# Layer 2's second half routed by rows of the batch, with layer 3's mixers, routes and experts queued in a new order behind it

## The chip, the cores and the metric

The kernel runs on one core of a Trainium2 chip, in one launch. The metric is the device time of an execution in microseconds (us), as the median of several runs. "The span" is the time between the first and the last event of one profiled execution. Times given as positions ("at 1664") are microseconds from the start of that span.

## The reference, cut to what matters

The input x has 4 batch rows of 1024 tokens with 128 features, in fp32. Four layers follow each other. Each layer is a mixer over tokens and then a feed-forward part (FFN), and behind each of the eight steps stands x = layernorm(x + step(x)). The change touches the last two layers:

```
# layer 2, mixer: causal attention with 16 heads of 8 features, inside one batch row
attn = softmax(where(tril, q @ k.T / sqrt(8), -inf));  out = (attn @ v) @ Wo.T + Wo_b
# layer 2, FFN: 8 experts (F = 512), the best 2 of each token by softmax(x @ gate_w.T)
# layer 3, mixer: over the FIRST axis (the 4 batch rows), for each token position by itself
n, b, e = query.shape                      # (4, 1024, 128)
x = query / (norm(query) * e ** -0.5 + 1e-8)
u = silu(x @ u_w.T + u_b);  v = silu(x @ v_w.T + v_b)          # 256 features, 8 heads
y = toeplitz over n of v (7 lags for each head)
out = (u * y) @ o_w.T + o_b + query
# layer 3, FFN: 32 experts (F = 128), the best 4 of each token, and one shared FFN (F = 512)
```

What matters for the order of the work: attention of layer 2 needs all earlier tokens of its own batch row, and no other row. The mixer of layer 3 needs all four batch rows at the same token position, and no other position. The FFNs work on each token alone.

## The kernel before, in words

**Tiles.** x stays on the chip's SBUF as 32 tiles of 128 tokens. They are kept in quarters of the sequence: a quarter is 256 tokens of each of the four rows, so 8 tiles (`tile_of`, `quarter`). A `Part` is a run of quarters: part a is quarters 0 and 1 (16 tiles), b is quarter 2 and c is quarter 3 (8 tiles each).

**Attention of layer 2** (`l2_attn(hf)`) runs in two halves of the sequence. Its second half goes row by row through the batch: 26 units for each row, each with score matmuls on TensorE, two exps on ScalarE (L1032, 128×1024 each) and value matmuls. The steps that close a row (`finish`: `turn`, `back`, `out`, `routed`, `logits`) and those that prepare the next row are put into a list `todo` and worked off between units. `logits` (L2's router) writes into `l2_lg`.

**An expert FFN** has these steps. A route (`l2_route`, `l3_route`, with `positions`, L1212 on) works out, mostly on VectorE (DVE), for each token the places in a list in DRAM sorted by expert. `spread` (L1280) has GpSimd (POOL) write each tile's x rows to those places by an indirect DMA, k per tile for the best k experts. `gathered` (L1294) loads groups of 512 list rows on SyncE's (SP's) queue, and waits for all scatters of the list. The experts (`l2_experts`, `small_experts`) multiply block by block with weights from one tile `wall`, loaded by `l2_wall` or `l3_wall`, and store the results to a second list. `collect` reads them back by k indirect gathers per tile on POOL (L1334) and adds them to x, weighted, on DVE (L1327). A list of layer 2 for 8 tiles has 24 blocks of 128 rows, that of layer 3 has 24 groups of 512 rows for part a and 16 each for b and c.

**Order.** All functions are generators, which yield an estimate of the microseconds that they have just queued. `mix(main, side)` (L210) advances the side by as many estimated microseconds as the main part has yielded. Side instructions are kept, by a dependency without a semaphore, behind the last instruction that the main part has queued on the same engine. What is left of the side when main is done is queued after it (`drain=True`) or is kept for the next mix (`drain=False`). Each engine works off its own queue in order. The scheduler of the framework may still move instructions without such a dependency within a queue. Tiles in SBUF come from pools on a stack at the left and one at the right edge. A tile that lies where a closed pool's tile was waits for the last use of that tile.

**The schedule from the second half of layer 2's attention on** (`all`, L1767 to L1781):

```python
run(self.mix(self.l2_attn(1), self.between(a, True)))
...
    routed = self.chain(self.routed(b), self.routed(c))
    run(self.mix(self.l3_experts(a, self.l3_wall(c2)), routed))
...
    run(self.mix(self.l2_experts(b, wall), self.last(a)))
    on = self.between(b)
    run(self.mix(self.l2_experts(c, wall), on, drain=False))
```

`between(part)` is layer 2's `collect`, then `l3_attn`, `l3_route` and `spread` of layer 3. So beside attention, part a goes through the rest of layer 2 and layer 3's mixer. Then part a's experts of layer 3 run, with the routing of layer 2's b and c beside them. Then come layer 2's experts of b (beside them `last(a)`, the gathers of layer 3's part a) and of c (beside them `between(b)`). Then layer 3 goes on for the rest: `l3_shared(a)`, shared and experts of b beside `between(c)`, shared and experts of c beside `finish(a)` (a layernorm and the stores of the output), `last(b)` and `finish(b)`; at the end `last(c)` and `finish(c)`. `l3_attn` has a form `exps`, used beside attention: it makes silu from Tanh and takes the square roots on DVE, so that ScalarE's exps keep their table. The plain form uses Silu and Sqrt on ScalarE.

Of the kernel before, what the change touches and what calls it, by code (L numbers as in the profile page):

```python
# [15 lines left out]
ALU = mybir.AluOpType  # L16
# [46 lines left out]
class Part:  # L63


    def __init__(self, name, q0, nq):
        self.name, self.q0, self.nq = name, q0, nq
        self.t0, self.nt = q0 * QT, nq * QT

    def tiles(self, x):  # L70
        return x[:, self.t0 : self.t0 + self.nt, :]
# [7 lines left out]
class Kernel:  # L79
    def __init__(self, ctx, tc, ins, out, cols, consts, rows):  # L80
# [34 lines left out]
        self.parts = (self.first, *self.rest)  # L115

        self.lists, self.route = {}, {}
        self.both = (self.first, Part("r", 2, 2))
        for lay, ne, k in (("l1", E1, K1), ("l2", E2, K2), ("l3", E3, K3)):
            for pt in self.both if lay == "l1" else self.parts:  # L120
                tl = -(-((pt.nt * P * k + (P - 1) * ne) // P) // 4) * 4
                self.lists[lay, pt.name] = (
                    self.tile(dram, [tl * P, D], f"{lay}r{pt.name}"), self.tile(dram, [tl * P, D], f"{lay}y{pt.name}"), tl
                )
# [19 lines left out]
    def load(self, pool, src, eng=None, tag=None):  # L144
        t = self.tile(pool, list(src.shape), tag or f"ld{next(self.count)}")
# [662 lines left out]
    def l1_close(self, part, yp):  # L808

        nc, x = self.nc, self.x  # L810
        for q in range(part.q0, part.q0 + part.nq):
            yield from self.collect("l1", part, K1, yp, part.tiles(x), (q - part.q0) * QT, QT)
# [43 lines left out]
    def l2_logits(self, ps, t4, lg, tag):  # L856
# [4 lines left out]
        self.nc.vector.tensor_copy(lg, pl.rearrange("p (q k) e -> p q k e", k=2))  # L861

    def l2_attn(self, hf):
# [6 lines left out]
        with ExitStack() as ctx:  # L870
            kv = self.pool(ctx, "l2kv")
            w = self.load(kv, self.ins["l2_w"])
# [15 lines left out]
            tp = self.pool(ctx, "l2t", 2)  # L888
# [49 lines left out]
            def finish(b, oc):  # L938
# [38 lines left out]
                def logits():  # L977
                    lg = self.l2_lg.rearrange("p (q b k) e -> p b q k e", q=NQT, b=B)[:, b, 2 * hf : 2 * hf + 2]
                    self.l2_logits(ps_m, made["t4"], lg, "s")
# [64 lines left out]
            def values_of(u, prs):  # L1044
# [13 lines left out]
                for m in [m for m in pos if ends[m][-1] == i]:  # L1058
                    t = self.tile(bp, [P, BLK], "oc", bufs=5)
# [41 lines left out]
            values_of(*late.pop(0))  # L1101
            for step in todo:
                step()
                yield (2.0,)
            if hf == 0:
                nc.sync.dma_start(out=self.vsave, in_=va)
                nc.sync.dma_start(out=self.ksave, in_=kT)

    def l2_attn_general(self):
# [3 lines left out]
        with ExitStack() as ctx:  # L1113
# [88 lines left out]
            for q in range(NQT):  # L1202
                self.norm(self.quarter(q))
                for g in range(2):
                    t0 = q * QT + g * 4
                    lg = self.l2_lg[:, t0 : t0 + 4, :].rearrange("p (q k) e -> p q k e", k=2)
                    t4 = self.tile(pp, [P, BLK], "t4")
                    self.transposes(ps_t, t4, [x[:, t0 + k, :] for k in range(4)], on_act=False)
                    self.l2_logits(ps_t, t4, lg, "tp")
# [64 lines left out]
    def spread(self, lay, part, k):  # L1274
# [3 lines left out]
        for t in range(part.nt):  # L1278
            for i in range(k):
                ins = self.nc.gpsimd.indirect_dma_start(  # L1280
                    out=rows, out_offset=bass.IndirectOffsetOnAxis(ap=pos[:, t, i : i + 1], axis=0),
                    in_=self.x[:, part.t0 + t, :], in_offset=None,
# [7 lines left out]
    def gathered(self, pool, rows, g, done):  # L1290
# [3 lines left out]
        ld = nc.sync.dma_start(out=xg, in_=rows[g * 4 * P : (g + 1) * 4 * P, :].rearrange("(t p) d -> p t d", p=P))  # L1294
        for o in done:
# [21 lines left out]
    def collect(self, lay, part, k, yp, acc, first=0, nt=None):  # L1317
# [7 lines left out]
        def add(t, yt):  # L1325
            for i in range(k):
                nc.vector.scalar_tensor_tensor(  # L1327
                    acc[:, t, :], yt[:, i, :], wk[:, t, i : i + 1], acc[:, t, :], ALU.mult, ALU.add
# [47 lines left out]
    def l2_route(self, part):  # L1376
        nc = self.nc
        with ExitStack() as ctx:
            cp = self.pool(ctx, "l2rc" + part.name, right=True)
            lg = part.tiles(self.l2_lg)  # L1380
# [17 lines left out]
    def l2_experts(self, part, wall):  # L1398
# [4 lines left out]
        with ExitStack() as ctx:  # L1403
            hp = self.pool(ctx, "l2fh" + part.name, 3)
# [3 lines left out]
            def inputs(g):  # L1408

                xg = self.gathered(hp, rows, g, done)  # L1410
# [17 lines left out]
            def turn(n):  # L1428
                h = gus.pop(n)
                hT = hTs[n] = self.tile(hp, [P, F2], "hT")  # L1430
# [37 lines left out]
    def l3_attn(self, part, exps=False):  # L1468

# [4 lines left out]
        with ExitStack() as ctx:  # L1474
# [5 lines left out]
            if exps:  # L1480
                hb = self.tile(cp, [P, 2 * NC], "hb")
                nc.vector.tensor_scalar(hb, col["l3_b"], 0.5, None, ALU.mult)

            def silu(dst, pz, i):

                if not exps:
                    nc.scalar.activation(dst, pz, AF.Silu, bias=col["l3_b"][:, i : i + 1])
                    return
                th = self.tile(vp, [P, BLK], "th", bufs=2)
                nc.scalar.activation(th, pz, AF.Tanh, bias=hb[:, i : i + 1], scale=0.5)  # L1490
                stt(dst, pz, col["l3_b"][:, i : i + 1], th, ALU.add, ALU.mult)
                stt(dst, pz, col["l3_b"][:, i : i + 1], dst, ALU.add, ALU.add)

            for q in range(part.q0, part.q0 + part.nq):
                s = slice(q * QT, (q + 1) * QT)
                self.norm(self.quarter(q), by="dve" if exps else "act")
# [3 lines left out]
                for g in range(2):  # L1500
# [5 lines left out]
                    if exps:  # L1506

                        ri = self.tile(self.small, [P, 4], "rmsi")
                        v = self.tile(self.small, [P, 4], "rmsv")
                        nc.vector.tensor_scalar(v, r, 1e-30, None, ALU.max)  # L1510
                        self.rsqrt(ri, v)
                        nc.vector.tensor_tensor(r, r, ri, ALU.mult)
                    else:
                        nc.scalar.activation(r, r, AF.Sqrt)
# [12 lines left out]
                for c in range(NC):  # L1527
                    v = self.tile(vp, [P, B, TQ], "v")
                    for i, dst in ((1, v), (0, u[:, c])):
                        for g in range(2):  # L1530
                            pz = self.tile(ps, [P, BLK], "s")
                            self.mm(pz, wuv[:, i, c * P : (c + 1) * P], xq[:, g * BLK : (g + 1) * BLK])
                            silu(dst[:, 2 * g : 2 * g + 2, :].rearrange("p b t -> p (b t)"), pz, i * NC + c)
                            yield (2.0 if exps else 1.5,)
# [428 lines left out]
```

## Time and profile before

| | |
|---|---|
| median of 6 runs | 2540.49 us (2530.13 to 2557.18) |
| the profiled execution's own time | 2541.02 us |
| its span | 2539.1 us |
| granted TensorE clock, mean | 0.824 |
| instructions | 28600 |
| second half of attention, first and last exp (L1032) | 1285.1, 1663.7 |
| scatters of layer 3's part a (L1280), first and last start | 1650.7, 1731.9 |
| layer 3's experts of a | 1748.5 to 1876 |
| layer 2's experts of b, of c | 1899 to 1998, 2007 to 2098 |
| layer 3's shared a | 2116 to 2166 |
| scatters of layer 3's part b, of c, first and last start | 2172.4 to 2211.9, 2337.9 to 2377.5 |
| layer 3's experts of b, of c | 2231 to 2308, 2402 to 2481 |
| last gathers (L1334), first and last start | 2485.2, 2524.0 |

How to read the profile: a row of "windows" gives, for a stretch of the span, the length, then the busy time and count of TensorE's matmuls (PE), its weight loads (PEld, which overlap the matmuls), VectorE (DVE), ScalarE (ACT) and GpSimd (POOL), then the granted clock as a share of full speed, the busy share of the DMA engines and what they moved. A row of "waits" names an engine, a tile and a line, then after the arrow what ended the wait, and the total, the count and the longest. Tiles are called by the program's names: `l3ra` is the list of rows of layer 3's part a, `l3ya` that of its results, `yt` what a gather brings back. Matmul ends are modelled, so a busy PE is not PE at its peak.

### The profile page before, as it was taken

How to read it: one execution, taken by the hardware profiler on the slowest of the kernel's cores; microseconds unless marked ns; L12 is line 12 of the kernel's file. 1: busy time of each engine (PE TensorE's matmuls, PEld its weight loads, DVE VectorE, ACT ScalarE, POOL GpSimd, SP SyncE). 2: the span in 40 equal slices, each digit the busy share in tenths (PEclk: the TensorE clock that was granted, in tenths of full speed). 3: DMA queues.
4: the chain of work that ended last, by engine and by line, in shares of the span. 5: the costliest groups of instructions: out<-in, count | busy, mean ns of one | idle time of the engine just before them, and what ended most of it. 6: DMA issues, size and time to landing. Idle time of an engine off the chain costs nothing.

```text
span 2539.1 us, 28600 instructions
## 1 busy us (share of the span) xinstructions
PE 1691.5 (67%) x9605; PEld 1035.7 (41%) x9605; DVE 1351.8 (53%) x3789; ACT 826.3 (33%) x1174; POOL 775.2 (31%) x725
## 2 busy tenths in 40 slices
PE   7538676873652874778887878835748796588180
PEld 3225333752320444645532323314635464275070
DVE  8864795855660653324545766623414463367153
ACT  5512363320320531212355555512312242053030
POOL 5432185236045004214130000072254401501614
PEclk9768787986775987888988999967869898799595
DMA  9902002321000122332210000015351203131242
GB/s 317 289 16 82 19 36 100 104 84 40 24 29 39 53 92 92 106 123 71 84 58 4 1 1 1 1 50 183 117 185 51 78 20 125 54 114 46 83 117 60
DMA packets 224439, 199.92 MB, mean 79 GB/s; under 512 B 16864, under 2 KB 204128, under 8 KB 223136
## 3 DMA queue, kind: packets, MB, share of 16 engines
q1 hardware_dynamic: 203584, 155.14, 19.2%
q0 software_dynamic: 20704, 42.86, 5.5%
q8 instruction: 83, 1.36, 0.2%
q14 instruction: 68, 0.56, 0.1%
HBM read 101.34 MB, written 96.60 MB: 78 GB/s over the span
## 4 chain that ended last, share of the span: by engine, by line
PE 35%; DVE 22%; POOL 14%; issue 11%; another core or an unknown queue 8%; DMA 5%; ACT 3%; SPq 0%; DVEq 0%; POOLq 0%; ACTq 0%
PE gu L150 10%; PE s L150 8%; POOL yt L1334 5%; PE yp L150 4%; PE tp L158 4%; PE sc L150 4%; POOL l1ra L1280 4%; POOL l3ra L1280 2%; DVE x L198 1%; DVE pr L1038 1%; DVE y L1545 1%; ACT pr L1032 1%; DVE s L341 1%; PE s L158 1%
## 5 line engine op out<-in xcount | busy, mean ns | idle before, releaser
L1032 ACT ACTIVATE pr<-sc 128x1024 f32<-128x1024 f32 x288 | 279.5, 1021 | 296.4 <-PE sc L150 209.4
L150 PE MATMUL gu<-ld,xgT 128*128 x768 | 212.6, 421 | 84.0 <-ACT xgT L160 44.5
L150 PE MATMUL s<-pr,va 128*32 128x512 f32 (+3 forms) x1536 | 169.4, 521 | 47.0 <-issue 23.8
L150 PE MATMUL sc<-qm,kT 32*128 32x512 f32 (+3 forms) x1536 | 195.6, 555 | 7.3 <-issue 4.0
L150 PEld LDWEIGHTS gu<-ld,xgT 128*128 128x128 f32 x768 | 150.2, 208 | 117.7 <-ACT xgT L160 66.4
L150 PE MATMUL gu<-wall,xgT 128*128 x352 | 176.9, 627 | 18.9 <-DMA xg<-l2ra 17.5
L1646 DVE TENSOR_TENSOR hg<-sg,gu 128x256 f32<-128x256 f32 x192 | 79.0, 416 | 165.2 <-ACT sg L1645 119.3
L1280 POOL DMA_INDIRECT l3ra<-x,posl3a x64 | 62.9, 983 | 334.1 <-DVE posl3a L1253 314.9
L160 ACT COPY xgT<-tp 128x512 f32<-128x512 f32 x118 | 69.1, 586 | 280.1 <-PE tp L158 184.1
L158 PE MATMUL tp<-ld,xg 128*128 128x128 f32 x472 | 79.4, 296 | 111.5 <-DMA out_x<-x 54.1
L162 DVE COPY hT<-tp 128x512 f32<-128x512 f32 x140 | 96.0, 685 | 90.6 <-PE tp L158 37.6
L1038 DVE TENSOR_TENSOR pr<-pr,ld 128x512 f32<-128x512 f32 (+1 forms) x160 | 91.6, 579 | 86.7 <-ACT pr L1032 80.9
L1645 ACT ACTIVATE sg<-gu 128x256 f32<-128x256 f32 x192 | 73.1, 384 | 189.4 <-PE gu L150 108.2
L158 PE MATMUL tp<-ld,hg 128*128 128x128 f32 x736 | 117.7, 282 | 24.4 <-DVE hT L162 18.4
L158 PEld LDWEIGHTS tp<-ld,hg 128*128 128x128 f32 x736 | 94.3, 146 | 82.1 <-issue 38.6
L150 PEld LDWEIGHTS sc<-qm,kT 32*128 32x128 f32 x1536 | 83.3, 195 | 107.6 <-issue 69.2
L1426 DVE TENSOR_TENSOR hg<-sg,gu 128x512 f32<-128x512 f32 x88 | 60.0, 682 | 115.4 <-ACT sg L1424 100.5
L1424 ACT ACTIVATE sg<-gu 128x512 f32<-128x512 f32 x88 | 52.6, 597 | 186.1 <-PE gu L150 140.9
L1280 POOL DMA_INDIRECT l1ra<-x,posl1a x64 | 93.8, 1465 | 60.2 <-DVE posl1a L1253 41.0
L158 PE MATMUL s<-ld,x 128*128 128x128 f32 x128 | 30.2, 353 | 120.8 <-DVE x L198 81.1
L1334 POOL DMA_INDIRECT yt<-l1yr,posl1r x64 | 60.6, 947 | 155.5 <-DVE x L1327 88.5
L158 PEld LDWEIGHTS tp<-ld,xg 128*128 128x128 f32 x472 | 59.5, 152 | 117.2 <-issue 89.9
(426 smaller groups left out, 3627.8 us busy)
## 6 DMA issues: line engine op xcount, KB each, us to landing
wall<-wall SPq DMA_DIRECT2D x16, 768.0 KB
ld<-in_l_w SPq DMA_DIRECT2D x2, 6144.0 KB
l3ra<-zero SPq DMA_DIRECT2D x1, 6144.0 KB
wall<-we SPq DMA_DIRECT2D x24, 256.0 KB
ld<-in_l_w SPq DMA_DIRECT2D x2, 3072.0 KB
xg<-l3ra SPq DMA_DIRECT2D x24, 256.0 KB
l3ya<-yg SPq DMA_DIRECT2D x24, 256.0 KB
l1ra<-zero SPq DMA_DIRECT2D x1, 5120.0 KB
```

What stands on the lines that cost most here:

```text
L150: return self.nc.tensor.matmul(out, lhsT, rhs, start=start, stop=stop)
L158: nc.tensor.transpose(pt[:, k * P : (k + 1) * P], s, self.ident)
L160: nc.scalar.copy(dst, pt[:, : n * P])
L162: nc.vector.tensor_copy(dst, pt[:, : n * P])
L1032: nc.scalar.activation(pr, sc[h], AF.Exp)
L1038: nc.vector.tensor_tensor(d, d, cst["tril"].unsqueeze(1).unsqueeze(1).to_broadcast([P, 2, n, P]), ALU.mult)
L1280: ins = self.nc.gpsimd.indirect_dma_start(out=rows, out_offset=bass.IndirectOffsetOnAxis(ap=pos[:, t, i : i + 1], axis=0), in_=self.x[:, p ...
L1334: nc.gpsimd.indirect_dma_start(out=yt[:, i, :], out_offset=None, in_=ys, in_offset=bass.IndirectOffsetOnAxis(ap=pos[:, t, i : i + 1], axis=0),
L1424: nc.scalar.activation(sg, gu[:, 0, :], AF.Silu)
L1426: nc.vector.tensor_tensor(h, sg, gu[:, 1, :], ALU.mult)
L1645: nc.scalar.activation(sg, pg[:, :, 0, :], AF.Silu)
L1646: nc.vector.tensor_tensor(h[:, 2 * c : 2 * c + 2, :], sg, pg[:, :, 1, :], ALU.mult)
```

## The change

It changes the order of the work from the second half of layer 2's attention on, and what that needs.

- `Part` gets `order`, a list of tiles. Layer 2's FFN now has the parts a2 (quarters 0 and 1, all rows), m (second half of rows 0 and 1) and n (second half of rows 2 and 3), of 16, 8 and 8 tiles. Layer 3 keeps a, b and c. The lists keep their sizes.
- Beside the second half of attention only the gathers of a2 (`rows_in`) run, and, once the logits of the second half's row 1 have been queued (`when`), the route and the 16 scatters of m.
- Then layer 2's experts of m and n run one behind the other under one `wall`. Beside them stand n's routing and layer 3's mixer, route and 64 scatters of part a (`onward`), without the `exps` form, which is removed.
- Then layer 3: what is left of part a's mixer is queued (`press`), the shared FFN of a writes into a tile `sh` through ScalarE (it was added to x by DVE) beside the rest of `onward(a)`, and `sh` is added to x by two DVE adds of 128×1024. The experts of a run beside the gathers of m and n and `onward(b)`; shared and experts of b beside `onward(c)`, `last(a)`, `finish(a)`; shared and experts of c beside `last(b)` and `finish(b)`; then `last(c)` and `finish(c)`, as before.
- In `l2_attn`, the pool `l2t` (weights `w`, and `rot`, `oc`, `o`, `oT`, `t4` of a row's finish) is opened first and stays open to the end. The other pools are closed before the last `todo` steps, and in the first half the keys' and values' stores move ahead of them.
- Single loads have one buffer, `hp` in `l2_experts` two in place of three (`hT` keeps three).

```diff
@@ l2_attn
-        with ExitStack() as ctx:
+        with ExitStack() as low, ExitStack() as ctx:
+            tp = self.pool(low, "l2t", 2)
+            w = self.load(tp, self.ins["l2_w"], tag="w")
             kv = self.pool(ctx, "l2kv")
-            w = self.load(kv, self.ins["l2_w"])
...
-            tp = self.pool(ctx, "l2t", 2)
...
-                    self.l2_logits(ps_m, made["t4"], lg, "s")
+                    self.l2_logits(ps_m, made["t4"], (hf * B + b) * 4, "s")
+                    self.rows_done += 1
...
             values_of(*late.pop(0))
+            if hf == 0:
+                nc.sync.dma_start(out=self.vsave, in_=va)
+                nc.sync.dma_start(out=self.ksave, in_=kT)
+            ctx.close()
             for step in todo:
                 step()
                 yield (2.0,)
@@ l3_shared
-                s = slice(blk * 4, blk * 4 + 4)
-                nc.vector.tensor_tensor(x[:, s, :], py, x[:, s, :], ALU.add)
+                if sh is None:
+                    s = slice(blk * 4, blk * 4 + 4)
+                    nc.vector.tensor_tensor(x[:, s, :], py, x[:, s, :], ALU.add)
+                else:
+                    t = blk * 4 - part.t0
+                    nc.scalar.copy(sh[:, t : t + 4, :], py)
@@ new
+    def when(self, ready):
+        while not ready():
+            yield (1.0,)
+
+    def rows_in(self, part):
+        with ExitStack() as ctx:
+            yp = self.pool(ctx, "l2y" + part.name, 5, right=True)
+            yield from self.collect("l2", part, K2, yp)
+
+    def onward(self, part):
+        yield from self.l3_attn(part)
+        self.mixed.add(part.name)
+        yield from self.l3_route(part)
+        yield from self.spread("l3", part, K3)
+
+    def press(self, side, ready):
+        while not ready():
+            next(side)
@@ all
-            run(self.mix(self.l2_attn(1), self.between(a, True)))
-            with ExitStack() as c2:
-                routed = self.chain(self.routed(b), self.routed(c))
-                run(self.mix(self.l3_experts(a, self.l3_wall(c2)), routed))
+            half = self.chain(self.rows_in(a2), self.when(lambda: self.rows_done >= B + 2), self.routed(m2))
+            run(self.mix(self.l2_attn(1), half))
             with ExitStack() as c2:
                 wall = self.l2_wall(c2)
-                run(self.mix(self.l2_experts(b, wall), self.last(a)))
-                on = self.between(b)
-                run(self.mix(self.l2_experts(c, wall), on, drain=False))
+                on = self.chain(self.routed(n2), self.onward(a))
+                run(self.mix(self.l2_experts(m2, wall), on, drain=False))
+                run(self.mix(self.l2_experts(n2, wall), on, drain=False))
             with ExitStack() as c2:
                 wall = self.l3_wall(c2)
-                run(self.mix(self.l3_shared(a), on))
-                on = self.between(c)
+                self.press(on, lambda: "a" in self.mixed)
+                hold = self.pool(c2, "l3hold")
+                sh = self.tile(hold, [P, a.nt, D], "sh")
+                run(self.mix(self.l3_shared(a, sh), on))
+                for q in range(a.nq):
+                    t = slice(q * QT, (q + 1) * QT)
+                    self.nc.vector.tensor_tensor(self.x[:, t, :], sh[:, t, :], self.x[:, t, :], ALU.add)
+                on = self.chain(self.rows_in(m2), self.rows_in(n2), self.onward(b))
+                run(self.mix(self.l3_experts(a, wall), on))
+                on = self.chain(self.onward(c), self.last(a), self.finish(a))
                 run(self.mix(self.chain(self.l3_shared(b), self.l3_experts(b, wall)), on))
-                run(self.mix(
-                    self.chain(self.l3_shared(c), self.l3_experts(c, wall)),
-                    self.chain(self.finish(a), self.last(b), self.finish(b)),
-                ))
+                on = self.chain(self.last(b), self.finish(b))
+                run(self.mix(self.chain(self.l3_shared(c), self.l3_experts(c, wall)), on))
             run(self.last(c), self.finish(c))
```

## The prediction, made before the changed kernel ran

> **What bounds the kernel now.** I read the page's busy line and chain first. TensorE is busy 67% of the span and the chain that ended last is 35% PE, 22% DVE, 14% POOL: no engine bounds the whole, so a change has to be priced stage by stage. I therefore asked for the busy time of each engine in windows cut at the stages from the second half of layer 2's attention (from 1260 us) to the end.
>
> ```profile
> core 0: us, PE busy (x) PEld busy (x) DVE busy (x) ACT busy (x) POOL busy (x), PEclk, DMA share, GB/s
> 1260.00:1665.00 405.00, 325.54 (x2393) 123.78 (x2397) 253.86 (x770) 217.93 (x233) 42.43 (x43) 0.92 0.06 19
> 1665.00:1748.00 83.00, 12.78 (x54) 8.70 (x47) 11.00 (x42) 0.10 (x1) 51.69 (x54) 0.53 0.32 128
> 1748.00:1876.00 128.00, 99.66 (x582) 87.33 (x580) 59.37 (x226) 45.55 (x91) 30.74 (x32) 0.85 0.36 107
> 1876.00:1899.00 23.00, 1.14 (x5) 0.77 (x5) 0.00 (x0) 0.59 (x1) 15.54 (x17) 0.54 1.02 362
> 1899.00:1999.00 100.00, 83.27 (x404) 53.51 (x404) 45.11 (x98) 23.47 (x41) 45.18 (x48) 0.94 0.21 54
> 2007.00:2098.00 91.00, 87.90 (x444) 57.35 (x443) 57.37 (x136) 37.84 (x60) 11.36 (x13) 0.98 0.15 43
> ...
> 2166.00:2231.00 65.00, 31.95 (x105) 18.61 (x104) 19.66 (x60) 5.31 (x9) 35.13 (x37) 0.70 0.20 66
> 2231.00:2308.00 77.00, 68.94 (x422) 58.30 (x420) 53.03 (x138) 41.04 (x76) 3.67 (x4) 0.99 0.35 103
> 2308.00:2402.00 94.00, 34.04 (x145) 22.57 (x146) 38.84 (x167) 12.99 (x19) 48.90 (x51) 0.66 0.20 62
> 2402.00:2481.00 79.00, 65.80 (x380) 57.31 (x378) 41.91 (x113) 29.82 (x60) 12.59 (x14) 0.88 0.40 113
> 2481.00:2540.00 59.00, 0.00 (x0) 0.00 (x0) 16.77 (x57) 1.37 (x2) 30.28 (x32) 0.54 0.21 54
> ```
>
> The reader sees four kinds of stretch. Attention takes 405 us. Experts stretches (128, 100, 91, 77, 79 us) are nearly full of matmuls. In gaps of 83, 65 and 94 us POOL scatters x rows for layer 3's parts a, b and c. At the end, 59 us, there is no matmul, only part c's gathers. The change rearranges just these.
>
> The second reading is who stops whom. In the windows of the scatters I asked for the waits (engine, line waited for: total us, times, longest). First the 64 scatters beside the first half of attention (730 to 825), then 16 scatters beside layer 3's experts (1844 to 1866):
>
> ```profile
> ACT pr L1032 <- remote: 71.5, 2, 69.7
> DVE t L162 <- remote: 59.9, 1, 59.9
> ```
>
> ```profile
> ACT sg L1645 <- remote: 13.1, 2, 10.0
> PEld gu L150 <- ACT xgT L160: 11.8, 2, 8.1
> ```
>
> "Remote" names no engine and no data queue. While scatters run, the other engines stand still: in the trace the instruction queues move no packet from 721 to 772 and from 1836 to 1865. So I price 16 scatters at 14 us of standstill beside attention and at 15 beside experts, not at nothing.
>
> The Trainium skill, "Runtime: NRT & Kernel Launch", section "Instruction fetch mechanics", says that crossing an instruction block costs one DMA tail-bump, mostly hidden. The 69.7 us wait speaks against it. By the rule the two moved scatter groups below cost nothing, and the sum would be 29 us lower.
>
> **The change, part by part** (us in the span; the profiled run took 2541.0 for a span of 2539.1, so 1.9 lies around it, and it stands 0.5 above the median 2540.5).
>
> 1. *Attention loses layer 3's mixer.* Its 52 exps (L1032) per row take 68 us in row 0 (1285 to 1353), where only gathers lie beside it, and 99, 103 and 95 in rows 1 to 3, where layer 3's mixer runs beside them. Its own lines take 76 us of DVE. Now rows 1 to 3 carry only the rest. A clean row is 68; rows 1 and 2 start with the next row's preparation and the finish of the last, about 11 us over their units in the first half (35 to 38 us against 25). I take 68+10=78; the bounds are 68 and 95. Routing m's 8 tiles and its 16 scatters come beside row 3: 14 us stall. Last exp: 1285+68+3×78+14, and about 6 for row changes = 1607; before 1664. Gain 57.
>
> 2. *First block of m.* The 48 KB weight tile now overlaps the attention's last tiles (pool l2t stands lowest and stays open through the last finish), so its load waits for row 3's logits. A row's finish took 17.4 us after its last exp in the first half (910.0 to 927.5), and the load took 23.4 (1875.6 issued, 1899.0 first matmul). 1607+17.4+23.4=1648. If the load could start earlier: up to 17 sooner.
>
> 3. *Experts m and n.* One part's 24 blocks at 3.05 are 73 us. Beside m lie n's routing and 16 scatters (15 us) and the first of layer 3's mixer on part a (9 us of PE), plus 6 at start: 103. Before, the same 24 blocks beside the gathers took 99.5, and c's took 91 beside the mixer on b (20 us of PE). N: 8 for the switch, 73+28 for the mixer = 109. End: 1648+103+109=1860. The mixer returns to ScalarE's Sqrt and Silu. Table loads are 1.28 us each; in part c's 91 us there were six of them and ACT was busy 37.8, so I count none on the path; the bounds are 0 and 16 loads × 1.28 = 21.
>
>    The Trainium skill, "ScalarE: Activation LUTs", section "What ACT_TABLE_LOAD costs", gives 1283 ns and a drain of 1380 ns with every switch. The first figure is the trace's. By the rule 16 switches are an estimated 43 us in place of 21, still on an engine with 53 idle us in such a stretch.
>
> 4. *Layer 3, part a.* What is left: wall and shared weight load (18 us idle before, 2098 to 2116), the rest of the mixer under `press` and the shared blocks (12.5 each before, 50 for four). One block is hidden behind the route, three are not: 18+32+12=62. pos a at 1922. Then 64 scatters at 1.27 (0.96+0.30 issue) = 82, and 11 for landing and first load (1731.9 to 1743.8): first expert of a 2015. Beside the scatters TensorE has only the last shared block: the 83 us gap returns whole, only later.
>
> 5. *Experts a.* 24 groups at 3.55 clean are 85 (it took 128 before with two scatter groups and their routes). Gathers of m and n (32) come beside it with layer 3's mixer on b (20 PE, partly hidden): 108, end 2123. The side's dues in the code add to 121 (2×24+73) against the experts' 92.5, so 28.5 are left over; I take half of them, since nothing else runs then: the mixer's last norm at 2137. Then pos b 22.5 later (row: c's x normed 2315.1, pos 2337.6) = 2160.
>
> 6. *Experts b.* 32 scatters × 1.27 + 12 = 53, with the shared blocks under them: 2213. The mixer on c runs beside: before, it was normed 84 after the stretch's start (2231, 2315.1), behind gathers that are now done earlier (16×1.25=20, partly ahead of it): +70, then pos c +22.5: 2306.
>
> 7. *The tail.* On POOL stand, in the order traced: 32 scatters of c, 64 gathers of a, 32 of b, 32 of c. Part a's gathers cannot start earlier: their buffers lie where layer 3's route of c keeps its tiles. 41+81+41+41, then 14 from the last gather to the end of stores (2525 to 2539.1), and about 10 of standing between groups (bounds 0 and the 35 that POOL waited for experts c's rows before): 2306+41+81+41+41+14+10=2534. Beside it, experts c: 53 after pos c (as in step 6), 87 (79 before, 8 for a's adds), 58 to the end: 198. So POOL, with 228, leads by 30. Before, a's 64 gathers lay beside experts b of layer 2, where POOL had time; that they are moved is the price of this change: 81.
>
> 8. *Small edits.* The hold tile adds two DVE adds of 128×1024; the nearest row is 128×512 at 0.58 (L1038), so 1.2 each. The lower end is 0, if they run under the scatters, which is where they stand: I take 0. Two list buffers in place of three (hp) in the layer 2 experts: at 3.05 a block, four blocks for one load of 2.9 us (1743.8 to 1746.7), so between 0 and 2.9 per part; I take 0, as the block is nearer full by PE (87.9 of 91).
>
> Sum: 2534+1.9 = **2536 us**, 0.2% under the profiled run.
>
> **The rivals.**
>
> *R1, the tail goes by experts c (faster).* If a's gathers run before c's scatters (8 of the gathers of layer 2's part c ran ahead of b's scatters in the trace, 2114.9 against 2172), POOL's 81 leave the chain. Experts c keep their 79 then, and the end is 2306+53+79+58+2=2498. Against it: the buffers of step 7. With ±18 for the start of step 7: 2480 to 2516.
>
> *R2, slower: a's gathers hold up experts c.* Their 64 adds stand on DVE in trace order ahead of experts c's products. If the DVE queue keeps them, each group of experts c waits for a's gathers. Experts c then go at POOL's pace: 78 of their own work and 81 of gathers, 159 in place of 87: 2306+53+159+58+2=2578. It decides from where experts c take more than 117 (87+30). For it: last(a)'s 64 gathers made the first of layer 2's stretches 100 instead of 78. Against it: then it was 22, not 81.
>
> *R3, slower: attention doesn't shorten, or not by this.* If rows hold at 90, the 57 shrink by 36: 2572. That the change doesn't do what it says is the same case: if `when` doesn't find row 1 ready in time, m's routing (22 us) and 16 scatters (21) drain after the attention, +45: 2581. Against: row 1's logits are traced about unit 14 of row 2, so 38 units are left, and the routing needs 50 us at 2.3 a unit, 22.
>
> **How the numbers follow.** My forecast gets 0.44, its own range 2512 to 2560 by the open terms of steps 1, 2 and 7 (±24). R1 0.27, R2 0.20, R3 0.09. About 0.5% (2527.8, 2553.2) is what measuring this kernel can tell from no change. My forecast gives 0.10 faster, 0.23 same and 0.11 slower. With R1 faster is 0.37, with R2 and R3 slower is 0.40, same 0.23. For 8 in 10 the range reaches a little under R1's middle and to the upper values of R2 and R3: 2492 to 2582.
>
> **What would show it.** Last exp (L1032) near 1607; first weight load of layer 2 only after row 3's logits, first product of m near 1648; last scatter of layer 3's a near 2004, nearly no matmul beside it; experts b from 2213; on POOL at the end the order c's scatters, a's, b's, c's gathers without gaps. Wrong if the last exp is past 1630 (step 1), if a's gathers lie before 2300 (R1), or if experts c take over 117 us (R2).

## The result and the profile after

Measured with the prediction, the changed kernel took 2538.48 us (2528.53 to 2547.1) and the kernel before 2540.56: ratio 0.9994, interval 0.998 to 1.0007, so no change. Two later measurements gave 0.9906 (0.9874 to 0.9937) and 0.9974 (0.9944 to 1.0005). The ratio lies between nothing and 1% faster. The forecast was 2536.

The number was right, but by luck and not by the working: two errors of some 50 us cancel. The prediction itself had given no change a chance of only 0.23. The windows of the changed kernel, cut at its stages (columns as in the prediction):

```profile
1260.00:1581.00 321.00, 293.25 (x2281) 111.94 (x2281) 131.14 (x376) 204.53 (x212) 46.44 (x48) 0.95 0.08 26
1581.00:1615.00 34.00, 8.67 (x52) 6.13 (x52) 9.78 (x40) 1.87 (x2) 0.00 (x0) 0.62 0.55 208
1615.00:1712.00 97.00, 83.83 (x410) 54.50 (x411) 45.09 (x149) 37.06 (x58) 15.37 (x16) 0.90 0.12 37
1712.00:1812.00 100.00, 93.21 (x481) 62.08 (x480) 63.86 (x159) 43.40 (x68) 0.00 (x0) 0.97 0.11 32
1812.00:1876.00 64.00, 53.56 (x219) 33.95 (x219) 44.25 (x163) 17.55 (x26) 0.00 (x0) 0.87 0.29 116
1876.00:1965.00 89.00, 14.03 (x80) 10.34 (x80) 13.84 (x22) 3.58 (x7) 68.21 (x69) 0.60 0.16 58
...
2168.00:2240.00 72.00, 69.51 (x441) 59.84 (x440) 50.19 (x130) 36.08 (x71) 0.00 (x0) 0.99 0.35 100
2240.00:2334.00 94.00, 30.10 (x124) 20.03 (x124) 27.41 (x100) 8.65 (x13) 52.11 (x54) 0.67 0.19 60
2334.00:2479.00 145.00, 74.06 (x377) 63.39 (x376) 65.09 (x214) 33.76 (x64) 70.72 (x74) 0.72 0.34 93
```

Attention's stretch is 84 us shorter (to 1581 in place of 1665), the gap with 64 scatters is back (1876 to 1965, PE 14 of 89), and experts b are clean (69.5 of 72). The row to look at is the last: experts c hold as much matmul work as before (74 against 66), but in 145 us in place of 79, and POOL is busy for half of it. The place of c's list (first scatter of c) came at 2256.5, 81 us sooner than before (2337.9). Experts c end where they ended before (2479, against 2481). So all that was gained upstream is lost between 2256 and 2479: the first product of experts c comes 78 us after c's first scatter (2334.4), where the forecast had 53, and from there experts c take 145 us where it had 87.

What POOL does there is told by its groups (start of first and last):

```profile
L1289 POOL DMA_INDIRECT l3rc<-x,posl3c x32: 956/962/1143, 2256.5 to 2296.1; - x32
```

```profile
L1345 POOL DMA_INDIRECT yt<-l3ya,posl3a x64: 942/947/1203, 2297.4 to 2392.3; - x64
...
L1345 POOL DMA_INDIRECT yt<-l3yb,posl3b x32: 942/947/948, 2395.6 to 2434.4; - x32
L1345 POOL DMA_INDIRECT yt<-l3yc,posl3c x32: 943/947/948, 2485.0 to 2523.7; - x32
```

The queue is that of the prediction: c's scatters, then a's, b's and c's gathers. But between b's and c's it stands still for 50 us (2435 to 2485), waiting for experts c. Two rows of the waits say how experts c were held, the first from 2240 to 2334, the second from 2334 to 2480:

```profile
DVE x L1595 <- remote: 29.3, 1, 29.3
```

```profile
ACT xgT L169 <- DVE x L1337: 53.6, 1, 53.6
...
ACT xgT L169 <- remote: 30.1, 4, 10.8
```

The copy of experts c's first inputs waits for an add of part a (L1337): that is order. "Remote" is something else: the view can't name the instruction that ended the wait. The packed trace says more. The 29.3 us and the four waits of 30.1 end with updates of a semaphore that only TensorE's instructions update, so the engines waited for TensorE, and its own record is missing there. The same holds for 31 of the kernel's 33 "remote" waits of over 3 us after the first 500 us of the span (418 of 430 us).

Does TensorE lack instructions? The DMA view of the same kernel from 2290 to 2362 shows no packet on the instruction queues q8 and q14; in the 72 us from 2170, in which POOL does nothing, there are six:

```profile
q0 software_dynamic: 1600, 3.28, 17.4%
q1 hardware_dynamic: 3168, 1.57, 7.6%
```

```profile
q1 hardware_dynamic: 13846, 6.82, 33.0%
q8 instruction: 4, 0.07, 0.4%
q14 instruction: 2, 0.02, 0.1%
```

That alone can't tell cause from effect: an engine that stands for another reason uses up no instructions either. Between 2362 and 2435, in which POOL issues 52 gathers, four packets move:

```profile
q14 instruction: 3, 0.02, 0.1%
q8 instruction: 1, 0.02, 0.1%
```

And the 29.3 us wait ended at 2329.6, without any packet between 2289.3 and 2362.1.

So there are two theories for the lost 80 us. **Order:** a's 64 adds stand on DVE ahead of experts c's own work, and carry experts c along with POOL (the prediction's R2). **Standstill:** while POOL issues one indirect DMA after another, TensorE hardly gets on, and with it those who wait for it, wherever the work stands in their queues. The expectations below give as its reason that the other engines get no instructions; that reason is not shown. A third question is where a's gathers should lie: *place*.

### The profile page after: what moved, and what is told of

Read it like the earlier page. It is cut to its first block, busy times and chain, and to the rows that moved or that the text cites. A ratio compares the mean times of both kernels' runs of the same rounds, so it can differ in the third digit from the quotient of the medians.

```text
span 2538.9 us, 28524 instructions
## 1 busy us (share of the span) xinstructions
PE 1687.4 (66%) x9605; PEld 1039.9 (41%) x9605; DVE 1303.7 (51%) x3634; ACT 846.6 (33%) x1199; POOL 778.3 (31%) x725
## 5 line engine op out<-in xcount | busy, mean ns | idle before, releaser
L159 PE MATMUL s<-pr,va 128*32 128x512 f32 (+3 forms) x1536 | 174.6, 518 | 41.9 <-issue 25.9
L159 PE MATMUL yp<-ld,hT 128*128 x768 | 103.4, 278 | 0.3 <-DVE hT L171 0.2
```

What stands on the lines that cost most here:

```text
L159: return self.nc.tensor.matmul(out, lhsT, rhs, start=start, stop=stop)
```

## The experiments

The first four kernels ran on a chip on which the kernel before takes 2280.5 us, all others on chips on which it takes 2547 to 2570, so a time is compared by its ratio to the kernel before on the same chip; where stages of two chips stand side by side, the text says so. On the quick chip row 1 of attention's first half, beside 64 scatters, takes 51 to 54 us in place of 126 to 128, and none of its four traces has a "remote" wait after the first 500 us of the span. In the other ten traces, those of over 3 us add up to 396 to 501 us, several engines counted together. The changed kernel itself was not run on the quick chip.

**a's gathers beside experts b.** They get a pool of their own and are woven by their estimates into the mixer and route of c; b's gathers are kept behind c's scatters.

```diff
-                on = self.chain(self.onward(c), self.last(a), self.finish(a))
-                run(self.mix(self.chain(self.l3_shared(b), self.l3_experts(b, wall)), on))
-                on = self.chain(self.last(b), self.finish(b))
+                with ExitStack() as c3:
+                    yp = self.pool(c3, "l3ya", 5, right=True)
+                    on = self.weave(self.onward(c), self.collect("l3", a, K3, yp))
+                    run(self.mix(self.chain(self.l3_shared(b), self.l3_experts(b, wall)), on, 0.5))
+                on = self.chain(self.finish(a), self.last(b), self.finish(b))
```

> The changed kernel, but part a's 64 gathers and adds of layer 3 lie beside experts b, woven into the mixer and route of c, and POOL's order at the end is scatters of b, gathers of a, scatters of c, gathers of b and of c. Place theory (what the change gained upstream is lost because a's gathers lie behind c's scatters, beside experts c): the positions of c stay near 2256, experts c take about 79 again in place of 145, and from there to the end it is 201 as in the kernel before (2337.9 to 2539.1): span 2457, with up to 22 more if a's gathers cost experts b what they cost layer 2's experts b in the kernel before (100 in place of 78): 2457 to 2480. Rival, lost to contention wherever they lie: the 64 gathers cost experts b and the mixer of c the same 66 that they cost experts c, the positions of c come at about 2320, span 2520 to 2540.

2211.7 beside 2280.5: 0.9708 (0.9679 to 0.9736). Place theory holds on the quick chip; its rival, contention, is hardly tested there. Experts c take 63 us, and b's stretch with all 64 gathers beside it is still filled by matmuls to 81% (86.6 of 107 us):

```profile
1933.00:2040.00 107.00, 86.64 (x489) 70.77 (x490) 82.65 (x268) 43.17 (x80) 65.50 (x65) 0.90 0.46 127
2040.00:2088.00 48.00, 18.93 (x90) 14.20 (x89) 18.05 (x69) 5.48 (x10) 36.45 (x38) 0.68 0.28 92
2088.00:2151.00 63.00, 58.79 (x375) 52.68 (x373) 41.83 (x113) 29.56 (x59) 24.72 (x26) 0.97 0.53 150
```

**a's gathers queued among experts c's instructions.** POOL's order stays; only the places in the other queues change.

```diff
-                on = self.chain(self.onward(c), self.last(a), self.finish(a))
+                on = self.onward(c)
                 run(self.mix(self.chain(self.l3_shared(b), self.l3_experts(b, wall)), on))
-                on = self.chain(self.last(b), self.finish(b))
+                on = self.chain(self.last(a), self.finish(a), self.last(b), self.finish(b))
```

> The changed kernel, but a's gathers and adds are queued among experts c's own instructions in place of all ahead of them. POOL's order is as in the changed kernel. Order theory (the adds stand ahead of experts c's products on DVE, the prediction's R2): experts c go at their own pace, done by about 2440, the last gathers follow POOL's queue, span about 2490. Standstill theory (while POOL issues indirect DMAs without a pause the other engines get no instructions, whatever their order): experts c still end near 2476, span 2530 to 2545.

2252.7 beside 2280.5: 0.9868 (0.9845 to 0.9891). Experts c take 76 us from their first to their last `gu` product, the first matmul of an expert (2079.8 to 2155.5; so below, where "first to last product" is said), and POOL runs through to the end with pauses of at most 2.5 us (c's first scatter 2032.9, last gather 2236.7, span 2251.9). Order theory holds on the quick chip.

**Pauses for POOL.** One buffer for the rows of a and b, adds at once.

```diff
-        AHEAD = 3
+        AHEAD = 0 if lay + part.name in ("l3a", "l3b") else 3
...
-            yp = self.pool(ctx, "l3y" + part.name, 5, right=True)
+            yp = self.pool(ctx, "l3y" + part.name, 5 if part.name == "c" else 1, right=True)
```

> The changed kernel, but the gathers of a and b at the end have one buffer in place of five and their adds follow at once, so POOL pauses after every 4 gathers until their rows have landed and been added: some 9 us a tile in place of 6, 24 tiles, so POOL's a and b gathers end at about 2513 in place of 2435 and the span is 2565 to 2575 by POOL alone. Order theory: experts c are carried along and end near 2510. Standstill theory: instructions are fetched in the pauses, experts c take about 100 to 115 from 2334 and end at 2435 to 2450, well before POOL's gathers of b.

1.0092 (1.0075 to 1.0108). From first to last product experts c take 111 us (2078.4 to 2189.2). That is as long as standstill theory expected, but they end with a's gathers (2188.6; b's end at 2247), as things would that are carried along by them. On the quick chip, which has little standstill, it decides nothing. The pauses themselves cost time: a's gathers take 116 us in place of 81.

**m's route after attention.**

```diff
-            half = self.chain(self.rows_in(a2), self.when(lambda: self.rows_done >= B + 2), self.routed(m2))
+            half = self.chain(self.rows_in(a2), self.when(lambda: self.rows_done >= 2 * B), self.routed(m2))
```

> The changed kernel, but m's route and 16 scatters wait until the logits of row 3 are queued, so that they come behind attention. By the prediction's price of 16 scatters beside attention (14 us of standstill) row 2 of attention takes 72 in place of 86, by what the trace of the changed kernel suggests 69; the last exp at 1563 to 1567. The first product of m then waits for route and scatters: logits 17 after the last exp, 22 for the route, 20 for the scatters, 12 to land: about 1634 to 1638 in place of 1615, span 2555 to 2562. If the scatters cost attention nothing, row 2 stays at 86 and the span is 2570 to 2580.

1.0068 (1.0052 to 1.0085). Row 2 takes 68.9 with no scatters beside it; with them it takes 72.1 in the other three kernels on this chip, so the 16 scatters cost 3.2 here. The tail of this kernel is the changed kernel's, and it shows order alone at work, from 2084 to 2235:

```profile
PE gu L159 <- DVE hg L1639: 61.8, 13, 23.2
...
DVE x L1337 <- DMA yt<-l3ya,posl3a: 60.9, 55, 17.5
```

DVE waits for gathered rows, and experts c's products wait for DVE behind it: they take 142 us (2088.7 to 2231.0) on the quick chip as well. With a's gathers queued among experts c, the same row of DVE's wait is 22.9.

**The changed kernel and the kernel before again.** No edit.

> The changed kernel as it is, beside the kernel before, since the kernel before took 2280 us in the last four comparisons and 2540 in the first measurement. From the run with m's route after attention (2296.7, whose first product of layer 2's m came 322.6 after attention's first exp, against 307.9 with m's route beside it): 2296.7-14.7=2282, ratio about 1.00. Order theory: experts c take about 146 here too, as in that run (2088 to 2234), though POOL's scatters hold up little here (row 1 of the first half 51 in place of 128). Standstill theory: without standstill experts c run clean, about 80, and the time is about 2250 (that of the run with a's gathers queued among experts c).

2540.9 beside 2561.4: 0.9906. The quick chip did not come up again, so what the changed kernel takes there stays open. Experts c, first to last product: 2334.1 to 2475.6, as in the first trace.

> The kernel before as it is, for its trace at 2280 us. If the missing 260 us are POOL's standstills, they are missing where POOL scatters or gathers without a pause beside other work: row 1 of attention's first half about 51 in place of 127.6, layer 3's experts a about 100 in place of 128, and stretches without POOL as long as before. If everything is faster by a tenth instead, each stretch is 0.9 of what it was, and attention's rows without company take 61 in place of 68.

One run, 2569.4: as in the first trace (row 1 128.3; experts a 1777.5 to 1902, 125 us), so it doesn't tell where the 260 us are. The traces of the changed kernel's variants on the quick chip do in part: their attention rows without company take the same 65 to 69 us and 64 scatters the same 82 us as elsewhere, while stretches with indirect DMAs beside work are shorter (row 1 51 in place of 128; layer 3's experts a with 32 gathers 91 in place of 113, first to last product). It isn't everything that is faster by a tenth.

**Twice the scatters.**

```diff
                 done.append(ins)
+                if lay + part.name == "l2m":
+                    extra = self.nc.gpsimd.indirect_dma_start(
+                        out=self.lists["l1", "r"][0],
+                        out_offset=bass.IndirectOffsetOnAxis(ap=pos[:, t, i : i + 1], axis=0),
+                        in_=self.x[:, part.order[t], :], in_offset=None,
+                    )
```

> The changed kernel with each of m's 16 scatters followed by a second one into a list that nobody reads, so 32 beside row 2 of attention, with no other work added. If the scatters themselves hold attention up, row 2's excess over 68.9 doubles: from 3.2 (72.1) to about 6.4 where POOL holds little, from 17.5 (86.4) to 35 where it holds much. If m's route on DVE holds it up, row 2 stays as it was, 72.1 or 86.4.

One run. Row 2 takes 68.9 without scatters, 88.5 with 16 (on the same chip) and 110.8 with 32, so it is the scatters and not m's route. They cost 1.2 to 1.4 us each, which is about POOL's time for one (0.96+0.30): while they run, attention hardly gets on. The windows of the exps, rows 1 to 3:

```profile
1359.00:1428.00 69.00, 50.27 (x52) 1.00 0.00 1
1428.00:1540.00 112.00, 51.10 (x54) 0.83 0.05 20
1540.00:1605.00 65.00, 49.94 (x52) 1.00 0.01 1
```

**The kernel before, with the mixer out of attention.**

```diff
-            run(self.mix(self.l2_attn(1), self.between(a, True)))
+            run(self.mix(self.l2_attn(1), self.last2(a)))
+            run(self.l3_attn(a, True), self.l3_route(a), self.spread("l3", a, K3))
```

(`last2` is the gathers of `between` alone.)

> The kernel before, but beside the second half of attention only the gathers; the mixer, route and scatters of layer 3's a come after attention. If the mixer was what made rows 1 to 3 take 95 to 104, they take 66 to 70 now, each. If a row costs its preparation and finish as the prediction took it, 78. If they stay at 95, it was something else (pools, the order of the steps) and the changed kernel's pools brought the gain. The whole is then about as long as before or up to 40 longer, since the mixer (some 70) runs with nothing beside it in place of some 100 gained.

Rows 1 to 3 take 68.9, 68.9 and 65.2 in place of 104.0, 106.2 and 100.8 (the kernel before on the same chip). So the mixer with its route made them long, and not the pools; this run doesn't tell which of the two. The whole takes 2614.4 beside 2561.4 (one run), 53 longer where at most 40 were expected.

**Both moves of a's gathers again, on a slow chip.**

> a's gathers queued among experts c's instructions, once more. At 2252.7 beside 2280.5 it was measured where 64 scatters hold row 1 of attention's first half to 51 us. Where that row takes 128, the two theories part. Order theory: experts c run at their own pace, about 80 to 100 in place of 142, and the span is by POOL's queue 2490 to 2505. Standstill theory: POOL issues 128 indirect DMAs nearly without a pause from the positions of c on, the other engines' instructions don't come, whatever their order, and experts c end near 2476 as in the changed kernel: span 2530 to 2545. If it is measured where that row takes 51, it repeats 0.987.

0.9872 (0.9853 to 0.9892), 2536.0 us. Neither theory by itself. Experts c take 88 us (2342.7 to 2430.4) in place of 142 in the changed kernel: order theory is right about them. But the ratio is little better than the changed kernel's on other chips (0.9906 to 0.9994), since POOL now becomes late: a's gathers take 126 us, against 81 on the quick chip. The waits from 2305 to 2480:

```profile
POOL yt L1345 <- DVE x L1337: 53.2, 7, 14.2
...
DVE x L1595 <- remote: 47.4, 1, 47.4
```

POOL waits for DVE's adds. In front of them DVE waits for a product of c's shared FFN (L1595 adds it to x): this wait too ends on TensorE's semaphore, at 2338.0. So standstill takes back what order gave.

> a's gathers beside experts b, once more. Where row 1 of attention's first half takes 128: place theory, as at 2211.7 beside 2280.5, a ratio of about 0.965 to 0.97, span 2457 to 2480. Standstill theory: the 64 gathers hold experts b and the mixer of c for as long as they held experts c, some 66, the positions of c come at 2300 to 2325 in place of 2256, and the span is 2500 to 2540, ratio 0.98 to 0.995. Where that row takes 51, it repeats 0.971.

0.9795 (0.9767 to 0.9823), 2516.2 us. In between: the positions of c come at 2303.5, within what standstill theory expects, but only 39 later than in the run before on the same chip (2264.7), where that theory had 66, and experts c run clean:

```profile
2164.00:2304.00 140.00, 94.69 (x492) 75.73 (x493) 83.92 (x269) 42.47 (x80) 62.68 (x66) 0.79 0.34 97
2304.00:2383.00 79.00, 17.95 (x84) 13.41 (x83) 19.10 (x68) 5.12 (x9) 49.34 (x52) 0.61 0.22 69
2383.00:2456.00 73.00, 61.31 (x376) 54.15 (x374) 42.10 (x113) 30.24 (x60) 11.36 (x12) 0.93 0.40 116
```

The stretch up to the positions of c is 140 us, against 107 on the quick chip: the gathers lie in time that isn't free.

**The same with pauses, and the changed kernel, on one slow chip.**

```diff
-        AHEAD = 3
+        AHEAD = 0 if lay + part.name == "l3a" else 3
...
-                    yp = self.pool(c3, "l3ya", 5, right=True)
+                    yp = self.pool(c3, "l3ya", 1, right=True)
```

> a's gathers beside experts b, as in the last run, but with one buffer in place of five and the adds at once, so POOL must pause after every 4 gathers until their rows are there and added (7.3 us a tile in place of 5, so 116 us in place of 81 by the run with pauses at 2301.5). Standstill theory, where attention's row 1 takes 128: the other engines get their instructions in the pauses, so experts b and the mixer of c are held less: the positions of c at 2275 to 2290 in place of 2303, ratio to before 0.970 to 0.976 in place of 0.9795. Rival (what holds them is the gathers' traffic or DVE's adds, not the missing pause): the positions of c at 2303 or later, ratio 0.979 or above. Where that row takes 51, POOL's longer 116 put off c's scatters by about 10: 0.975 in place of 0.971.

> The changed kernel as it is, for its ratio beside the others on the same chip. Where attention's row 1 takes 128: experts c about 142 from first to last product, ratio 0.990 to 1.000, as in the two measurements there. Where it takes 51: by order theory experts c take about 146 all the same, time about 2282 beside 2280, ratio 0.998 to 1.004; if the loss at the end needs the standstill, experts c take about 80 and the ratio is 0.985.

With pauses 2509.1 beside 2547.2: 0.9846 (0.9798 to 0.9894); the changed kernel beside it 2537.0, 0.9974. The positions of c come at 2298.7, not 2275 to 2290, and 47 later than in the changed kernel on this chip (2252.2); the ratio is the rival's. a's gathers take 122 us with one buffer and 121 with five: with five, POOL stood for DVE's adds anyway (42.2 us in the run before), so the edit gave few pauses that weren't there. That pauses help is not shown. That the place helps is, here together with the single buffer: 27.8 us on the same chip, 1.1% below the changed kernel. a's gathers beside experts b is the best version found: it beats the kernel before on all three chips on which it ran, with or without pauses, and the changed kernel on the one where both ran.

## Why the prediction was right, and where it was not

Its steps against the profile of the changed kernel (us; a stage runs from the end of the one above):

| step | forecast | measured | off by |
|---|---|---|---|
| 1. last exp | 1607 | 1581 | -26 |
| 2. to first product of m | 41 | 34 | -7 |
| 3. experts m and n | 212 | 197 | -15 |
| 4. to positions of a | 62 | 64 | +2 |
| 4. scatters, to first product | 93 | 89 | -4 |
| 5. experts a, to positions of b | 145 | 157 | +12 |
| 6. to first product of b | 53 | 47 | -6 |
| 6. to positions of c | 93 | 88 | -5 |
| 7. tail | 228 | 282 | +54 |

**Step 1 was mis-sized.** That attention loses the mixer, and that this gives rows of 68 us, is shown twice (the changed kernel; the kernel before without the mixer). The 10 us that I added for each row's preparation and finish, and the 6 for row changes, are not there: rows 1 and 3, without scatters, take 65 to 69 and follow each other within 0.4 us. Against this gain, the first exp came 6 us later than before (1291.3 against 1285.1). The price of m's scatters, 14, is 17.5 (86.4 against 68.9) in the first trace.

**Steps 2 to 6** hold as a sum, with 15 us too much on the second layer's experts and 12 too little on experts a and what follows them. In step 4 the terms 32 and 12 have no row behind them; that 62 was met by 64 says little about them. The first product of m did wait for the weight load behind row 3's last steps, in 34 us. The scatters of n cost 13 in the products of m (1650.3 to 1663.6, no product), near the forecast 15. ScalarE's table loads in experts m and n are exactly the 16 that I took as the upper bound, and still not on the path: the stretch was shorter than forecast, not longer. The two DVE adds (1.2 us each) wait for a's scatters and run with them, as step 8 said; two buffers for three can't be seen in any stage.

**Step 7 failed**, and R2 stands in its place. The forecast had POOL carry the tail in one run of 160 operations, 228 us from the positions of c, with about 10 of standing between the groups (bounds 0 and 35) and experts c done 30 us before. It took 282: from a's first gather to b's first went 98 in place of 81, and before c's gathers POOL stood for 50. With a's gathers queued among experts c on the quick chip, POOL does carry the tail as forecast: 219 us from c's first scatter to the end. In the changed kernel experts c took 142 us, first to last product, more than the 117 from which R2 decides. R2's reason, the order on DVE, is shown (142 to 76 us on the quick chip, 142 to 88 off it). Its price, 159, was a little high. What R2 lacked is the second half: the standstill, which the prediction had priced for scatters beside attention and layer 2's experts, but not in the tail. There the first product of experts c comes 78 us after c's first scatter in all traces with this tail off the quick chip, and 47 on it (forecast 53), and POOL's own gathers are slowed through DVE. So R2's sum for the tail, 270, came near 282 by two errors of its own.

R1's point, that a's gathers might run ahead of c's scatters, did not happen: they started 0.3 us behind them, and with a pool of their own they started 0.3 us behind b's. That fits step 7, but whether it was the buffers that held them or their place in the program is not shown, since the run with a pool of their own moved both. R3 fell: m's route was reached in row 2, and its scatters ran from 1485.7.

The standstill was weighed against the Trainium skill, "Runtime: NRT & Kernel Launch", section "Instruction fetch mechanics", by which the fetch of the next block is mostly hidden. The runs neither show this nor speak against it. The prediction held its 69.7 us wait against it, but that wait ended at 812.2 on TensorE's semaphore, behind POOL's last scatter (ended 806.9) and before the next packet (817.6). Of 27 "remote" waits of over 5 us in the changed kernel, after the first 500 us, one ended within 3 us after an instruction packet. The size of the standstill is measured: 17.5 us for 16 scatters in the first trace, 41.9 for 32 on another chip, 3.2 for 16 on the quick one. What holds TensorE, and why the chips differ, no run here shows.

So the expected gain went this way: attention gave 84 us, of which 81 were still there at the positions of c, and the move of `last(a)` out of layer 2's experts and into the tail took them back: by order, shown on the quick chip and on another one, and off the quick chip by standstill too.

## What to carry to other kernels

Before work is moved, look for what it leaves behind: the side work that used to lie there (here 64 gathers) needs another place, and at the end of the kernel, beside experts c, it was dearer than beside experts b. An in-order engine that adds gathered rows carries along everything queued behind these adds, so put side work among the main work's instructions or ahead of the stretch that it would hold. Price a run of indirect DMAs as time of TensorE and of all that waits for it, until a trace shows other work going on beside it. And where a view calls a wait "remote", ask what ended it before giving it a cause.

## What the runs showed of the hardware

On most chips here, a run of indirect scatters without a pause holds TensorE up for about as long as it lasts (1.2 to 1.4 us for each scatter, beside attention), and the engines that need its products wait with it. TensorE doesn't stop at once: in row 1 of attention's first half, in the kernel before, its recorded matmuls start 2 to 3 us apart from 758 to 788, and the next record is at 816. On one chip out of four with their own measurement of the kernel before, 16 scatters cost 3.2 us, no wait after the first 500 us ends "remote", and the kernel before takes 2280.5 us in place of 2547 to 2570. Instruction packets come among POOL's DMAs on that chip as on the others (four from 2362 to 2435 above). Here they are in the kernel with a's gathers queued among experts c's instructions, from 2074 to 2146 on the quick chip:

```profile
q0 software_dynamic: 1840, 3.80, 22.1%
q8 instruction: 3, 0.05, 0.3%
q14 instruction: 3, 0.02, 0.1%
```

Gathers beside experts were less costly than scatters beside attention, 0.6 to 0.7 us each against 1.2 to 1.4: 64 gathers beside experts b, about 81 us of issue, put off the positions of c by 39 us on one chip (2303.5 against 2264.7) and by 47 on another (2298.7 against 2252.2). That POOL's waits for its buffers make the difference is not shown.
